# Gated products of two feed forwards in 512 columns instead of 256, on one Trainium2 core

## The chip, the cores and the metric

The kernel runs on one NeuronCore of one Trainium2 chip. The metric is the device time of one execution in microseconds (us). Five engines work side by side: PE (matmuls; PEld is its weight load), DVE and ACT (elementwise work, both can read the matmul banks), POOL (elementwise work on SBUF alone) and SP, which here issues every DMA.

## The reference

A two-layer transformer block on `x` of 128 sequences x 32 tokens x 256 features, with a context of 128 x 257 x 256. Each of the six steps adds to `x`, after a layer norm:

```python
x = x + L0_xattn(ln(x), ctx)      # 16 heads, 257 context tokens, biases, RMS norm of q and k
x = x + L0_attn(ln(x))            # differential attention with rotary positions
x = x + L0_ffn(ln(x))             # C: silu(x @ w1.T) * (x @ w2.T) @ w3.T, 704 features, weights through NF4
x = x + L1_xattn(ln(x), mask, ctx)  # 32 heads, self part and context part
x = x + L1_attn(ln(x))            # 16 heads of 16, causal
x = x + L1_ffn(ln(x))             # F: 8 experts, all applied, weighted by a router
# L1_ffn: gate = x @ Wg[e]; up = x @ Wu[e]; h = silu(gate) * up; out = sum_e w[e] * (h @ Wd[e]), 256 features
```

silu(a) is computed as a * (1 + tanh(a/2)) / 2, the halving being folded into later factors.

## The kernel before

The tokens are cut into 32 groups of 128 (4 sequences). Each step of the reference is a Python generator over groups: `A_prep`, `rowpass` (maxima of the scores, written to `mx`), `pvpass` and `pv` (exponentials `P`, their remainders `Pl`, products with `V`, copies `Uc`), `attn_fin`, `B_gen`, `C_gen`, then `D_prep`, `D_self`, the same `rowpass`/`pvpass`/`attn_fin` for layer 1, `E_gen`, `E_att` (the last attention, in tiles of 32x32 of the matmul array), `F_gen` and `F_down`. `C_gen` and `F_gen` take two groups at a time, so 256 tokens, 16 times each.

Numbers are kept to more than half precision by pairs: a value and its remainder, each in 16 bits. So a feed forward's hidden tile `hid` is written in float32, its upper halves are read as bfloat16, and POOL subtracts them from `hid` to give the remainder (`hidl` in C, `fhl` in F).

**What sets the order.** A planner (`pipeline`, `Stream.step`, `Est`) advances the generators one step (one `yield`) at a time, always the one with the smallest key. `Est.note` places each instruction into the first hole of its engine's estimated timeline after its operands are ready, with estimated costs from `Est.cost`. At the end every engine's instructions are sorted by estimated start, and that order is pinned for PE, ACT, DVE, POOL and the DMAs. The planner also counts matmul columns in stretches of `TICK` (3413 ns): where a stretch lacks columns (under `WARM` = 3060, pro rata), the streams in `HEAVY` (`ctx`, `F`, `Fd`) are pulled ahead, else held back.

**Banks.** PE writes eight banks of 128 x 512 float32. `tk()` gives a step the bank that is estimated to be free first; a step may take several.

**The gated products.** In F (`F_gen`) each expert has two feature tiles of 128. For each, 12 matmuls of 256 columns fill one bank: gates in columns 0 to 255, ups in 256 to 511. Then

```python
nc.scalar.activation(t, ps[:, :256], AF.Tanh, scale=0.5 * IWS)
nc.vector.scalar_tensor_tensor(t, t, 1.0, ps[:, :256], ALU.add, ALU.mult)
nc.vector.tensor_tensor(hid[:, ft], t, ps[:, 256:512], ALU.mult)
nc.gpsimd.tensor_tensor(hl[:, ft], hid[:, ft], hid.bitcast(BF)[:, ft, 1::2], ALU.subtract)
```

with `t` the tile `glu_t` of 128 x 256 float32 (two buffers). Each tile is one step of the stream. `F_down` multiplies `hid` and `hl` by the expert's third matrix (two times 6 matmuls of 256 columns) and adds into `xt`; it runs as a stream of its own, at most two experts behind. C is alike with 6 feature tiles (five of 128 and one of 64), 8 matmuls per tile, and its down product in the same generator.

All instructions are recorded by one helper, so every line of the profile names L290, and groups are told apart by the names of their tiles.

Of the kernel before, what the change touches and what calls it, by code (L numbers as in the profile page):

```python
# [12 lines left out]
F32 = mybir.dt.float32  # L13
F16 = mybir.dt.float16
BF = mybir.dt.bfloat16
AF = mybir.ActivationFunctionType
ALU = mybir.AluOpType
# [17 lines left out]
IWS = 1.0 / WS  # L35
# [55 lines left out]
FT = [128] * 5 + [64]  # L91
# [274 lines left out]
class Body:  # L366
# [140 lines left out]
    def ln_T(self, xts, pool, tag=None):  # L507
        nc = self.nc
        n = len(xts)
        mv = self.sm.tile([128, 2, 2], F32, name="bmv")  # L510
        for t in range(n):
            st = self.sm.tile([128, 6], F32, name="bst")
            nc.vector.bn_stats(st, xts[t])
            nc.vector.bn_aggr(mv[:, t, :], st)
        rs = self.sm.tile([128, 2], F32, name="brs")
        self.rsqrt(rs[:, :n], mv[:, :n, 1], 1e-5)
        hs = []
        nm = self.sm.tile([128, 2], F32, name="bnm")
        for t in range(n):
            nc.gpsimd.tensor_scalar(nm[:, t:t + 1], mv[:, t, 0:1], rs[:, t:t + 1], -1.0, ALU.mult, ALU.mult)  # L520
            h = pool.tile([128, 256], F32, name=f"lnh{t}", tag=tag, bufs=tag and n)
            nc.scalar.activation(h, xts[t], AF.Identity, bias=nm[:, t:t + 1], scale=rs[:, t:t + 1])
            hs.append(h)
        yield "end"
        ps = self.tk()
        for t, h in enumerate(hs):
            for k in range(2):
                nc.tensor.transpose(ps[:, (k * n + t) * 128:(k * n + t) * 128 + 128], h[:, k * 128:k * 128 + 128], self.ident)
        hT = pool.tile([128, 2, 2, 128 * n], F16, name="hT")
        self.split_ps(ps[:, :256 * n], hT[:, 0].rearrange("p k t -> p (k t)"), hT[:, 1].rearrange("p k t -> p (k t)"))  # L530
        return hT
# [624 lines left out]
    def setup_C(self):  # L1156
        nc, T = self.nc, self.T
        yield from self.need(("set", "A"))
        w1T = [self.w0.tile([128, 2, 704], BF, name=f"ffn{i}") for i in range(2)]
        self.w12T = w1T  # L1160
        self.w3T = self.w0.tile([128, 6, 256], BF, name="ffn3")
        w3d = self.dr.tile([88 * 2048], BF, name="w3d")
# [2 lines left out]
        for wi in range(3):  # L1165
# [3 lines left out]
            a = self.nf.tile([88, 32], F32, name="nfa")  # L1169
# [3 lines left out]
            ps = self.tk()  # L1173
# [25 lines left out]
            sc = self.nf.tile([88, 2048], BF, name="nfs")  # L1199
# [4 lines left out]
            for n in range(4):  # L1204
                ps = self.tk()
# [7 lines left out]
            if wi < 2:  # L1213
                for k in range(2):
                    ps = self.tk().bitcast(BF)
                    for r in range(8):
                        nc.tensor.transpose(ps[:, r * 88:r * 88 + 88], wq[:, r * 256 + k * 128:r * 256 + k * 128 + 128], self.identb[:88, :88])
                    nc.vector.tensor_copy(w1T[wi][:, k, :].rearrange("p (s r) -> p r s", r=8), ps[:, :704].rearrange("p (r s) -> p r s", r=8))
                    yield "end"
            else:  # L1220
                nc.sync.dma_start(w3d.rearrange("(p n) -> p n", p=88), wq)
                w3 = self.nf.tile([128, 2, 704], BF, name="nfw3", tag="nfs")
                nc.sync.dma_start(w3, w3d.rearrange("(k p f) -> p k f", k=2, p=128))
                for ft in range(6):
                    ps = self.tk().bitcast(BF)
                    for k in range(2):
                        nc.tensor.transpose(ps[:FT[ft], k * 128:k * 128 + 128], w3[:, k, ft * 128:ft * 128 + FT[ft]], self.identb)
                    nc.vector.tensor_copy(self.w3T[:FT[ft], ft, :], ps[:FT[ft], :256])
                    yield "end"

    def C_gen(self, g):
        nc = self.nc
        yield from self.need(("B", 2 * g), ("B", 2 * g + 1), ("set", "C"))
        xts = [self.xt[2 * g], self.xt[2 * g + 1]]
        hT = yield from self.ln_T(xts, self.cw, "glu_t")
        yield "end"
        hid = self.cw.tile([128, 6, 256], F32, name="hid")
        hl = self.cw.tile([128, 6, 256], F16, name="hidl")
        for ft in range(6):
            n = FT[ft]  # L1240
            ps = self.tk()
            for u in range(2):
                seq = [(k, a) for k in (0, 1) for a in (0, 1)]
                for i, (k, a) in enumerate(seq):
                    nc.tensor.matmul(ps[:n, u * 256:u * 256 + 256], self.w12T[u][:, k, ft * 128:ft * 128 + n], hT[:, a, k, :], start=(i == 0), stop=(i == 3))
            t = self.cw.tile([128, 256], F32, name="glu_t", bufs=2)
            nc.scalar.activation(t[:n], ps[:n, :256], AF.Tanh, scale=0.5)
            nc.vector.scalar_tensor_tensor(t[:n], t[:n], 1.0, ps[:n, :256], ALU.add, ALU.mult)
            nc.vector.tensor_tensor(hid[:n, ft], t[:n], ps[:n, 256:512], ALU.mult)
            nc.gpsimd.tensor_tensor(hl[:n, ft], hid[:n, ft], hid[:n].bitcast(BF)[:, ft, 1::2], ALU.subtract)  # L1250
            yield "pe" if ft < 5 else [hl]
        hv = hid.bitcast(BF)
        for tt in range(2):
            ps = self.tk()
            for ft in range(6):
                n = FT[ft]
                nc.tensor.matmul(ps[:, :256], hv[:n, ft, 1 + tt * 256:tt * 256 + 256:2], self.w3T[:n, ft, :], start=(ft == 0), stop=False)
                nc.tensor.matmul(ps[:, :256], hl[:n, ft, tt * 128:tt * 128 + 128], self.w3T[:n, ft, :], start=False, stop=(ft == 5))
            nc.vector.scalar_tensor_tensor(xts[tt], ps[:, :256], 0.5, xts[tt], ALU.mult, ALU.add)
            yield "pe"  # L1260
# [302 lines left out]
    def F_gen(self, g):  # L1563
        nc = self.nc
        yield from self.need(("E", 2 * g), ("E", 2 * g + 1), ("set", "F"))
        xts = [self.xt[self.NH + 2 * g], self.xt[self.NH + 2 * g + 1]]
        hT = yield from self.ln_T(xts, self.fw, "glu_t")
        w = self.router(hT)
        yield [hT]
        for e in range(8):  # L1570
            yield from self.need(*[("Fd", g * 8 + e - 2)] * (g * 8 + e > 1))
            hid = self.fw.tile([128, 2, 256], F32, name="fhid", bufs=2)
            hl = self.fw.tile([128, 2, 256], F16, name="fhl", bufs=2)
            for ft in range(2):
                ps = self.tk()
                for u, nm in enumerate((f"wg{e}", f"wu{e}")):
                    self.mm_feat(ps[:, u * 256:u * 256 + 256], self.W[nm], ft * 128, 128, lambda k: hT[:, 0, k, :], lambda k: hT[:, 1, k, :])
                t = self.fw.tile([128, 256], F32, name="glu_t", bufs=2)
                nc.scalar.activation(t, ps[:, :256], AF.Tanh, scale=0.5 * IWS)
                nc.vector.scalar_tensor_tensor(t, t, 1.0, ps[:, :256], ALU.add, ALU.mult)  # L1580
                nc.vector.tensor_tensor(hid[:, ft], t, ps[:, 256:512], ALU.mult)
                nc.gpsimd.tensor_tensor(hl[:, ft], hid[:, ft], hid.bitcast(BF)[:, ft, 1::2], ALU.subtract)
                yield "pe"
            self.fh[g * 8 + e] = (hid, hl, w)
            self.mark("Fu", g * 8 + e)

# [190 lines left out]
```

## Time and profile before

| | |
|---|---|
| median of 3 runs | 3372.8 us (3371.24 to 3373.25) |
| the profiled execution | 3372.91 us, its span 3371.1 us |
| mean granted PE clock | 0.937 of full speed |
| busy: PE, DVE, ACT, POOL | 3022.6, 2451.2, 2246.3, 2104.3 us |
| tanh of 256 columns (ACT, `glu_t`) | 352, 134.7 us |
| scalar_tensor_tensor (DVE, `glu_t`) | 352, 145.1 us |
| product (DVE, `fhid` and `hid`) | 256 and 96 |
| subtraction (POOL, `fhl` and `hidl`) | 256 and 96 |

In a line of the profile, "out<-in shape xcount" is followed by the busy time of the group in us, the mean ns of one, and after the second bar the idle time of the engine just before these instructions with what ended most of it. In windows, each engine has its busy us and its instructions in brackets; after the engines come the granted clock of PE, the share of DMA and GB/s.

### The profile page before, as it was taken

The numbers are of one execution on the slowest core, as the hardware profiler recorded it, in microseconds if no ns is written. First come the engines' busy times: TensorE is split into PE (matmuls) and PEld (weight loads), VectorE is DVE, ScalarE is ACT, GpSimd is POOL, SyncE is SP. The second block draws the span as 40 slices with busy tenths as digits, with TensorE's granted clock in tenths as the row PEclk, the third lists the DMA queues.
The fourth block names the chain that finished last, engine by engine and source line by source line (L and its number), as shares of the span: only waits on it lengthen the run. The fifth ranks groups of instructions, "written<-read, shape, count | busy, mean of one in ns | idle before, by whom it ended". The sixth has DMA issues, their size and how long they took to land. (4 is left out here: it accounts for less than half of the span.)

```text
span 3371.1 us, 106946 instructions
## 1 busy us (share of the span) xinstructions
PE 3022.6 (90%) x41537; PEld 2271.9 (67%) x41537; DVE 2451.2 (73%) x6084; ACT 2246.3 (67%) x6477; POOL 2104.3 (62%) x2537
## 2 busy tenths in 40 slices
PE   3888999999999999998777999889989889989899
PEld 1455776666766666665555777667777777777677
DVE  4787666766667666666767778777888788787866
ACT  2455888878887787786666656666676666656562
POOL 1354787777777777775454756556666656656463
PEclk9899999999999999999876999889999899988889
DMA  4565777777777777776565444544454445445420
GB/s 105 156 178 156 207 220 213 223 214 209 217 222 215 220 204 206 211 219 168 142 163 135 111 107 98 126 111 113 110 133 100 121 106 123 107 98 122 107 60 14
DMA packets 687849, 511.64 MB, mean 152 GB/s; under 512 B 224396, under 2 KB 675340, under 8 KB 687340
## 3 DMA queue, kind: packets, MB, share of 16 engines
q1 hardware_dynamic: 687340, 504.80, 55.1%
q8 instruction: 326, 5.34, 0.7%
q14 instruction: 183, 1.50, 0.2%
HBM read 319.86 MB, written 180.19 MB: 148 GB/s over the span
## 5 line engine op out<-in xcount | busy, mean ns | idle before, releaser
L290 POOL TENSOR_TENSOR Pl<-P 128x512 f16<-128x512 f32 x768 | 805.9, 1064 | 241.3 <-ACT P L290 232.4
L290 DVE TENSOR_REDUCE mx<-bank 128x2 f32<-128x512 f32 x768 | 479.8, 679 | 28.2 <-PE bank L290 25.2
L290 ACT ACTIVATE P<-bank 128x512 f32<-128x512 f32 x768 | 438.6, 599 | 89.1 <-PE bank L290 63.1
L290 ACT COPY Uc<-bank 32x68 f32<-32x68 f32 x1536 | 314.7, 205 | 108.0 <-PE bank L290 88.3
L290 DVE TENSOR_TENSOR vv<-bank,vv 128x256 f16<-128x256 f32 x512 | 215.2, 424 | 145.2 <-ACT vv L290 139.7
L290 POOL TENSOR_TENSOR fhl<-fhid 128x256 f16<-128x256 f32 x256 | 156.5, 612 | 250.2 <-DVE fhid L290 238.8
L290 ACT CAST vv<-bank 128x256 f16<-128x256 f32 x512 | 203.3, 402 | 156.9 <-DVE vv L290 84.9
L290 PE MATMUL bank<-V,P 128*128 128x68 f16 (+1 forms) x4096 | 295.5, 197 | 10.4 <-DVE mx L290 3.9
L290 PE MATMUL bank<-V,Pl 128*128 128x36 f16 (+1 forms) x3072 | 280.8, 191 | 11.3 <-POOL Pl L290 9.3
L290 PEld LDWEIGHTS <-Kst 97*128 97x128 f16 x4096 | 232.8, 100 | 78.1 <-issue 51.2
L290 PEld LDWEIGHTS <-P 128*128 128x128 bf16 x4096 | 258.1, 100 | 24.5 <-issue 7.9
L290 ACT ACTIVATE glu_t<-bank 128x256 f32<-128x256 f32 x352 | 134.7, 383 | 192.3 <-PE bank L290 170.1
L290 PEld LDWEIGHTS <-Pl 128*128 128x128 f16 x3072 | 235.0, 98 | 37.0 <-POOL Pl L290 21.8
L290 DVE SCALAR_TENSOR_TENSOR glu_t<-glu_t,bank 128x256 f32<-128x256 f32 x352 | 145.1, 412 | 116.4 <-ACT glu_t L290 115.2
L290 PEld LDWEIGHTS <-ch 128*128 128x128 f16 x2048 | 191.7, 99 | 56.1 <-issue 27.2
L290 PE MATMUL bank<-QstD,Kst 97*128 97x128 f16 x2048 | 200.4, 228 | 27.8 <-DVE rbt L290 5.5
L290 PEld LDWEIGHTS <-hT 128*128 128x128 f16 x1536 | 138.5, 102 | 107.7 <-issue 30.5
L290 POOL TENSOR_TENSOR kk<-kb,kk 128x512 f16<-128x512 f32 x128 | 146.0, 1160 | 94.0 <-ACT kk L290 92.7
L290 PE MATMUL bank<-khf,eh 32*128 32x256 f16 (+1 forms) x1536 | 162.7, 284 | 46.4 <-DVE mx L290 10.2
L290 POOL TENSOR_TENSOR cl<-ct,ch 128x1024 f16<-128x1024 f32 x64 | 136.6, 2135 | 44.8 <-ACT ch L290 42.7
L290 DVE SCALAR_TENSOR_TENSOR xt<-bank,w,xt 128x256 f32<-128x256 f32 x256 | 120.0, 472 | 21.5 <-PE bank L290 20.1
L290 PEld LDWEIGHTS <-eh 32*128 32x128 f16 (+1 forms) x1536 | 53.1, 93 | 121.9 <-issue 107.9
(483 smaller groups left out, 9098.2 us busy)
## 6 DMA issues: line engine op xcount, KB each, us to landing
Kst<-kd SPq DMA_DIRECT2D x384, 256.0 KB
kd<-kk SPq DMA_DIRECT2D x128, 512.0 KB
vd<-vv SPq DMA_DIRECT2D x256, 136.0 KB
V<-vd SPq DMA_DIRECT2D x64, 544.0 KB
vd<-vv SPq DMA_DIRECT2D x256, 132.0 KB
V<-vd SPq DMA_DIRECT2D x64, 528.0 KB
ct<-in_ctxm SPq DMA_DIRECT2D x64, 512.0 KB
khf<-kd SPq DMA_DIRECT2D x128, 256.0 KB
```

The source lines that it names most:

```text
L290: r = f(*a, **k)
```

## The change

The gates of two feature tiles go into one bank and their ups into another; so tanh, the two steps on DVE and the subtraction on POOL handle 512 columns at once. F then has one step of 24 matmuls per expert instead of two of 12, C three of 16 instead of six of 8. C's sixth feature tile becomes a full one: the transposed weights get 768 columns, of which the last 64 are set to zero by two memsets; its down product reads 64 rows as before. The three instructions move into a helper `glu`. The tiles `glu_t` (and the layer norm's `lnh`, which shares their buffers) grow to 512 columns, and the scratch for dynamic DMAs is set to 8192 bytes.

```diff
-            h = pool.tile([128, 256], F32, name=f"lnh{t}", tag=tag, bufs=tag and n)
+            h = pool.tile([128, 512], F32, name=f"lnh{t}", tag=tag, bufs=tag and n)[:, :256]
...
-        w1T = [self.w0.tile([128, 2, 704], BF, name=f"ffn{i}") for i in range(2)]
+        w1T = [self.w0.tile([128, 2, 768], BF, name=f"ffn{i}") for i in range(2)]
+        for t in w1T:
+            nc.vector.memset(t[:, :, 704:], 0.0)
...
+    def glu(self, t, ps, out, sc):
+        nc = self.nc
+        nc.scalar.activation(t, ps[0], AF.Tanh, scale=sc)
+        nc.vector.scalar_tensor_tensor(t, t, 1.0, ps[0], ALU.add, ALU.mult)
+        nc.vector.tensor_tensor(out, t, ps[1], ALU.mult)
...
 # C_gen
-        for ft in range(6):
-            n = FT[ft]
-            ps = self.tk()
+        for f2 in range(3):
+            f = slice(2 * f2, 2 * f2 + 2)
+            ps = [self.tk() for _ in range(2)]
             for u in range(2):
...
+                for ft in range(2):
+                    seq = [(k, a) for k in (0, 1) for a in (0, 1)]
+                    for i, (k, a) in enumerate(seq):
+                        nc.tensor.matmul(ps[u][:, ft * 256:ft * 256 + 256], self.w12T[u][:, k, (2 * f2 + ft) * 128:(2 * f2 + ft) * 128 + 128], hT[:, a, k, :], start=(i == 0), stop=(i == 3))
+            t = self.cw.tile([128, 512], F32, name="glu_t", bufs=2)
+            self.glu(t, ps, hid[:, f].rearrange("p f t -> p (f t)"), 0.5)
+            nc.gpsimd.tensor_tensor(hl[:, f], hid[:, f], hid.bitcast(BF)[:, f, 1::2], ALU.subtract)
+            yield "pe" if f2 < 2 else [hl]
...
 # F_gen
-            for ft in range(2):
-                ps = self.tk()
-                for u, nm in enumerate((f"wg{e}", f"wu{e}")):
-                    self.mm_feat(ps[:, u * 256:u * 256 + 256], self.W[nm], ft * 128, 128, lambda k: hT[:, 0, k, :], lambda k: hT[:, 1, k, :])
...
+            ps = [self.tk() for _ in range(2)]
+            for u, nm in enumerate((f"wg{e}", f"wu{e}")):
+                for ft in range(2):
+                    self.mm_feat(ps[u][:, ft * 256:ft * 256 + 256], self.W[nm], ft * 128, 128, lambda k: hT[:, 0, k, :], lambda k: hT[:, 1, k, :])
+            t = self.fw.tile([128, 512], F32, name="glu_t", bufs=2)
+            self.glu(t, ps, hid.rearrange("p f t -> p (f t)"), 0.5 * IWS)
+            nc.gpsimd.tensor_tensor(hl, hid, hid.bitcast(BF)[:, :, 1::2], ALU.subtract)
+            yield "pe"
...
-    nc = bacc.Bacc("TRN2", target_bir_lowering=False, num_devices=1)
+    nc = bacc.Bacc("TRN2", target_bir_lowering=False, num_devices=1, dynamic_dma_scratch_size=8192)
```

More of the change, by code (lines that the diff above doesn't have):

```diff
@@ L1217, in setup_C @@
                         nc.tensor.transpose(ps[:, r * 88:r * 88 + 88], wq[:, r * 256 + k * 128:r * 256 + k * 128 + 128], self.identb[:88, :88])
-                    nc.vector.tensor_copy(w1T[wi][:, k, :].rearrange("p (s r) -> p r s", r=8), ps[:, :704].rearrange("p (r s) -> p r s", r=8))
+                    nc.vector.tensor_copy(w1T[wi][:, k, :704].rearrange("p (s r) -> p r s", r=8), ps[:, :704].rearrange("p (r s) -> p r s", r=8))
                     yield "end"
@@ L1238, in C_gen @@
         hl = self.cw.tile([128, 6, 256], F16, name="hidl")
-        for ft in range(6):
-            n = FT[ft]
-            ps = self.tk()
+        for f2 in range(3):
+            f = slice(2 * f2, 2 * f2 + 2)
+            ps = [self.tk() for _ in range(2)]
             for u in range(2):
[L1243 to L1251, printed above, removed]
+                for ft in range(2):
[6 more added lines that the diff above has]
+            yield "pe" if f2 < 2 else [hl]
         hv = hid.bitcast(BF)
@@ L1573, in F_gen @@
             hl = self.fw.tile([128, 2, 256], F16, name="fhl", bufs=2)
-            for ft in range(2):
-                ps = self.tk()
-                for u, nm in enumerate((f"wg{e}", f"wu{e}")):
-                    self.mm_feat(ps[:, u * 256:u * 256 + 256], self.W[nm], ft * 128, 128, lambda k: hT[:, 0, k, :], lambda k: hT[:, 1, k, :])
[L1578 to L1583, printed above, removed]
+            ps = [self.tk() for _ in range(2)]
[6 more added lines that the diff above has]
+            yield "pe"
             self.fh[g * 8 + e] = (hid, hl, w)
```

## The prediction

> **What bounds the kernel now.** I read the page's busy line first, then the windows by stage, then one-microsecond windows, then the groups that the change touches, then DVE's order of time. The page:
>
> ```profile
> PE 3022.6 (90%) x41537; PEld 2271.9 (67%) x41537; DVE 2451.2 (73%) x6084; ACT 2246.3 (67%) x6477; POOL 2104.3 (62%) x2537
> ```
>
> PE leads, but 90% is an average. The windows by stage (PE, PEld, DVE, ACT, POOL busy, then the granted clock) part it:
>
> ```profile
> 400.00:1500.00 1100.00, 1058.91 (x11821) 762.34 (x11820) 740.96 (x1890) 880.32 (x2483) 830.55 (x970) 0.99 0.73 215
> 1500.00:1800.00 300.00, 236.54 (x2984) 167.71 (x2984) 207.11 (x462) 194.00 (x568) 159.25 (x195) 0.82 0.62 162
> 1800.00:3330.00 1530.00, 1390.29 (x23749) 1118.05 (x23748) 1203.55 (x2988) 963.23 (x2878) 924.11 (x1162) 0.92 0.44 106
> 3330.00:3371.10 41.10, 34.42 (x312) 28.56 (x309) 26.43 (x86) 7.95 (x22) 10.20 (x18) 1.00 0.04 14
> ```
>
> From 400 to 1500 (attention of layer 0 with the first feed forward, C) PE sets the pace: 41 us idle, full clock. From 1800 to 3330 (layer 1, with the experts, F) PE loses 140 us idle, and 113 us more to a lower clock (its busy time times one less the clock, summed over one-microsecond windows). DVE is 79% busy there, and not evenly: in 674 of the 1530 one-microsecond windows it is at 0.97 or more, and 72 of the 140 and 55 of the 113 us fall in these. Four windows in a row show how:
>
> ```profile
> 2413.00:2414.00 1.00, 0.45 (x4) 0.17 (x4) 1.00 (x3) 0.95 (x5) 1.00 (x1) 1.00 0.31 66
> 2414.00:2415.00 1.00, 0.73 (x4) 0.23 (x4) 1.00 (x2) 1.00 (x4) 0.05 (x1) 1.00 0.31 68
> 2415.00:2416.00 1.00, 0.78 (x8) 0.69 (x8) 1.00 (x3) 0.60 (x2) 0.00 (x0) 0.92 0.27 63
> 2416.00:2417.00 1.00, 1.00 (x6) 0.70 (x5) 0.90 (x3) 0.00 (x0) 0.22 (x1) 0.50 0.82 187
> ```
>
> DVE is full, PE waits for its maxima (0.45, 0.73), and then PE's clock is halved. The lower clock comes in 40 stretches of 3.4 us or small multiples, 251 us in all: 74 pieces of 3.4 us, each costing 113/74 = 1.5 us. So one DVE queue costs twice.
>
> **The change part by part.** Per expert, two tanh, two scalar_tensor_tensor, two products and two POOL subtractions of 256 columns become one each of 512; C's 96 become 48 likewise. The durations, from the page's groups:
>
> ```profile
> L290 POOL TENSOR_TENSOR Pl<-P 128x512 f16<-128x512 f32 x768 | 805.9, 1064 | 241.3 <-ACT P L290 232.4
> ...
> L290 ACT ACTIVATE P<-bank 128x512 f32<-128x512 f32 x768 | 438.6, 599 | 89.1 <-PE bank L290 63.1
> ...
> L290 POOL TENSOR_TENSOR fhl<-fhid 128x256 f16<-128x256 f32 x256 | 156.5, 612 | 250.2 <-DVE fhid L290 238.8
> ...
> L290 ACT ACTIVATE glu_t<-bank 128x256 f32<-128x256 f32 x352 | 134.7, 383 | 192.3 <-PE bank L290 170.1
> ...
> L290 DVE SCALAR_TENSOR_TENSOR glu_t<-glu_t,bank 128x256 f32<-128x256 f32 x352 | 145.1, 412 | 116.4 <-ACT glu_t L290 115.2
> ```
>
> and DVE's groups by form:
>
> ```profile
> L290 DVE TENSOR_TENSOR fhid<-glu_t,bank 128x256 f32<-128x256 f32 x256 | 107.3, 419 | 11.9 <-DVE glu_t L290 0.5
> L290 DVE SCALAR_TENSOR_TENSOR kk<-bank,kk 128x512 f16<-128x512 f32 x128 | 86.4, 685 | 24.9 <-ACT kk L290 24.4
> ```
>
> *DVE.* By durations an expert falls from 2x(412+419) = 1662 to 685+680 = 1365 ns (680: products of 512 from a bank), 297 less. Where DVE is full, neighbours overlap, so the time from start to start counts (start, duration):
>
> ```profile
> 2511.37 0.41 DVE L290 SCALAR_TENSOR_TENSOR glu_t<-glu_t,bank 128x256 f32<-128x256 f32 x1
> 2511.81 0.42 DVE L290 TENSOR_TENSOR fhid<-glu_t,bank 128x256 f32<-128x256 f32 x1
> 2512.15 0.68 DVE L290 TENSOR_TENSOR qkT<-bank,qkT 128x512 f16<-128x512 f32 x1
> 2512.75 2.47 DVE L290 TENSOR_REDUCE mx<-bank 128x2 f32<-128x512 f32 x4
> ```
>
> A pair takes 2512.15 - 2511.37 = 0.78 us. At 512 the first needs 0.685 + 0.03 (the second depends on it, as here) and the second 0.60 (qkT's start to the next): 1.315. Two old pairs less one new is 0.245 us. If all overlapped by 0.06 (mx: 4 in 2.47, where one lasts 0.68) it would be 0.18; if nothing did, 0.30. I take 0.245, measured on these very instructions. 120 experts lie before 3330: 29 us. On the path goes the share of windows in which DVE is full, 674/1530 = 44%: **13 us** (10 to 16 by the bounds; all 36 if DVE paced the whole stage).
>
> *ACT.* 2x383 - 599 = 167 ns, 120 times: 20 us. ACT is at 0.95 or more, DVE not being full, in 262 of 1530 windows: **3.5 us**. Two tanh one after the other took 0.81 us, no less than 2x0.383, so I count nothing off. [...]
>
> *POOL.* 2x612 - 1064 = 160 ns, 120 times: 19 us. Full alone in 197 of 1530 windows: **2.5 us**.
>
> *The other stages.* C saves the same per pair of tiles on engines that PE outruns in need: DVE is full in 314 of its 1100 windows, but PE lost only 10 us in those. **1 us** (0 to 5). 1500 to 1800: PE's largest waits there are for mx (9.9 us), QstD's load (4.9) and weights (4.3), none of which the change touches: 0. The last 41 us are paced by PE (34.4 busy): tanh and the first product now run beside the ups' matmuls, after which product and subtraction take 0.68+1.06 against 0.38+0.41+0.42+0.61 for the last tile before: 0, within 0.5.
>
> *PE and the banks.* The matmuls are as many and as wide (C's sixth tile now has 128 rows for 64; rows do not show in the durations, 606 against 612 ns in POOL's subtraction). One tile took 12 matmuls, 1.3 us, in one bank; now 24, 2.6 us, in two banks at once. Bank time per expert, without queueing: 2x(1.3+0.38+0.41+0.42) = 5.0 us before; gates 1.3+0.60+0.68 and ups 1.3+0.68 after, 4.6. No new shortage. A new wait is possible where the first down matmul, which could start on the first tile's half, now needs both: PE waited 15.4 us for fhid in this stage. I keep that sum. Behind the longer tanh stand P's exponentials, behind the longer subtraction Pl's; neither new piece is longer than those, so nobody's worst wait grows.
>
> *Coarser filling.* The planner pulls F ahead when PE's current 3.4 us lack columns. It had 256 pieces of 3072 columns for that, now 128 of 6144, of which one may fill a stretch twice and leave the next thin. Below by nothing (a piece spread over two stretches serves both); above, 20 more slow pieces, 30 us. I take 3 pieces, **4.5 us** against the change, near the lower end, since matmuls are placed one by one into holes. [...]
>
> *Less thin time.* If a lighter DVE queue spares 2 of 74 slow pieces (DVE's load falls by 29/1204 = 2.4%): **3 us**.
>
> *Memsets and scratch.* Two small memsets in the start-up: under 0.5 us on DVE. [...]
>
> Sum: 13+3.5+2.5+1+3-4.5 = 18.5 us. The profiled execution took 3372.9 us (span 3371.1), the median is 3372.8, so nothing is to be converted: **3354 us**.
>
> **The rivals.** *Slower by clumps.* Every engine's order is written out from the planner's estimates, so all of it is dealt anew, and F's doubled pieces leave more thin stretches. For: the clock falls on thin windows, not on gaps; F and its down products are the only filler in this stage. Against: estimates are placed matmul by matmul. Against 23 us of gain at 1.5 us each, 15 more slow pieces (on 74) cancel the change, and from 20 it is slower. At 30: 3373-23+45 = 3395 us. *Nothing.* In DVE's full windows PE is still 89% busy (72 of 674 idle); the freed time goes to waits for P and Uc on ACT (15.2 and 11.4 us of PE's waits), and the new order scatters it: 3371 us. *More.* Full DVE windows set off the slow clock; if 20 of 74 slow pieces go, 30 us on top of 18: 3325 us. *Not as said:* if the ups' first matmul waited for the second bank to be drained, PE would show waits ahead of wu; the 4.6 against 5.0 us speaks against it.
>
> **How the numbers follow.** Forecast (3335 to 3366) 0.45, more 0.12, nothing 0.14, clumps 0.29. The measurement can tell about 0.2%, 6.7 us, from no change: faster 0.57, same 0.14, slower 0.29. The range runs from 3322 (DVE's 36 us, ACT, POOL and 3 slow pieces) to 3394 (some 30 slow pieces more); a tenth is left out on each side. The faster cases alone: 3325 to 3366.
>
> **What would show it.** Right: tanh near 600, both DVE forms near 680, POOL near 1060 ns, 176 each; DVE's sum in F's stage down by 30 to 36 us at equal PE busy; fewer full DVE windows; PE waits for mx below 15.7 us. Wrong: a clock under 0.92 from 1800 to the tail with more half-clock stretches; PE waits for fhid well over 15.4 us; or a longer 400 to 1800, where I expect no change.

## The result, and the profile after

After the change the kernel takes 3401.5 us (median of 6 runs, 3390.8 to 3409.4) against 3372.0: a ratio of 1.0087, 95% interval 1.0067 to 1.0107, so 29 us slower. The profiled execution took 3390.8 us, its span is 3389.0 us. The page's busy line:

```profile
PE 3032.6 (89%) x41537; PEld 2284.1 (67%) x41537; DVE 2397.2 (71%) x5734; ACT 2227.7 (66%) x6301; POOL 2081.5 (61%) x2361
```

The relief is there: DVE has 54 us less, ACT 19, POOL 23, with 350, 176 and 176 fewer instructions. The groups have the forecast durations (597, 680 and 1040 ns, 176, 176 and 128 of them):

```profile
L290 POOL TENSOR_TENSOR fhl<-fhid 128x512 f16<-128x512 f32 x128 | 133.1, 1040 | 215.0 <-DVE fhid L290 208.0
...
L290 ACT ACTIVATE glu_t<-bank 128x512 f32<-128x512 f32 x176 | 104.9, 597 | 103.8 <-PE bank L290 89.4
L290 DVE SCALAR_TENSOR_TENSOR glu_t<-glu_t,bank 128x512 f32<-128x512 f32 x176 | 119.7, 680 | 74.5 <-ACT glu_t L290 73.6
```

The windows by stage (columns as before) show where the time went nevertheless:

```profile
400.00:1500.00 1100.00, 1066.19 (x12058) 772.69 (x12055) 743.45 (x1842) 890.93 (x2480) 842.72 (x951) 1.00 0.75 218
1500.00:1800.00 300.00, 237.33 (x3063) 168.97 (x3060) 198.18 (x441) 194.56 (x577) 158.21 (x189) 0.80 0.62 158
1800.00:3330.00 1530.00, 1379.01 (x23113) 1107.28 (x23114) 1147.90 (x2706) 931.11 (x2697) 886.52 (x1017) 0.90 0.44 104
3330.00:3389.00 59.00, 47.24 (x620) 38.76 (x617) 32.45 (x86) 9.81 (x20) 13.12 (x15) 0.88 0.06 15
```

Until 1500 us the kernel is a little ahead (237 more matmuls than before in the stretch from 400 us, clock 1.00 for 0.99), and at 1800 us it leads by 328. In layer 1 it falls back: in the same 1530 us, 636 fewer matmuls, with a clock of 0.90 for 0.92. Summed over one-microsecond windows from 1800 to 41 us before the end, PE sat idle 157 us (before 140) and ran 308 us at half clock (before 251), although DVE is at 75% where it was at 79%. The cost of the lower clock, summed as in the prediction, is 133 us there for 113. Together that is 37 us lost in layer 1; with the lead at 1800 us, the profiled execution ends 18 us later than the one before (it is the fastest of the six).

What happens is seen in the one-microsecond windows around 2757 us, after the change (PE, PEld, DVE, ACT, POOL, clock, then the share of DMA and GB/s):

```profile
2756.00:2757.00 1.00, 0.76 (x5) 0.20 (x5) 0.93 (x5) 0.33 (x2) 0.63 (x1) 1.00 0.00 0
2757.00:2758.00 1.00, 0.00 (x0) 0.00 (x0) 0.83 (x6) 0.00 (x0) 0.00 (x0) 1.00 0.00 0
2758.00:2759.00 1.00, 0.04 (x1) 0.04 (x2) 0.87 (x3) 0.00 (x0) 0.00 (x0) 1.00 0.19 68
2759.00:2760.00 1.00, 0.58 (x4) 0.14 (x3) 0.99 (x2) 0.00 (x0) 0.22 (x1) 1.00 0.18 64
2760.00:2761.00 1.00, 0.77 (x6) 0.60 (x5) 1.00 (x3) 0.00 (x0) 0.81 (x1) 0.75 0.00 0
2761.00:2762.00 1.00, 1.00 (x7) 0.70 (x5) 1.00 (x3) 0.00 (x0) 0.00 (x0) 0.50 0.61 206
```

and in PE's order of time (start, duration; in brackets the idle time ahead and what ended it):

```profile
2754.18 0.38 PE L290 MATMUL bank<-hT,wu0l 128*128 128x256 f16 x2
...
2756.03 0.73 PE L290 MATMUL bank<-khf,eh 32*128 32x256 f16 x4
2758.96 0.37 PE L290 MATMUL bank<-khf,eh 32*128 32x256 f16 x2 [2.19 <-DVE glu_t L290]
2759.75 0.37 PE L290 MATMUL bank<-khf,eh 32*128 32x256 f16 x2 [0.42 <-DVE fhid L290]
2760.35 0.91 PE L290 MATMUL bank<-hT,wg1h 128*128 128x256 f16 x4 [0.23 <-DVE mx L290]
```

The last ups of expert 0 (`wu0l`) ran at 2754; then `rowpass` (khf) waits for the bank that held that expert's gates until DVE, busy with the router's small steps, has read it at 2758. No matmul of F stands in the order until `wg1h` at 2760, so nothing fills the gap; the granted clock goes from 1.00 to 0.50 at 2760.5 us, and the next 24 matmuls begin under it (the row of two `wg1l` at 2761.05 reads 0.63 us, that of two `wu0l` at 2754.18 0.38).

One place proves little, so I counted this over layer 1. From PE's order of time, cut into 448 stretches of 3.41 us from 1800 us, 150 had no gate or up matmul before; after, 241. And this absence goes with the clock: of 38 falls of the clock in layer 1 before, 20 had no matmul of F (gates, ups or down) in the 4 us ahead, while only 10% of all full-clock microseconds have that; after, 28 of 44, and 16% of all.

PE's waits in layer 1 (total us, times, longest), two of them before:

```profile
PE bank L290 <- DVE fhid L290: 15.4, 15, 2.6
PE bank L290 <- DMA QstD<-ed: 1.9, 2, 1.4
```

and after:

```profile
PE bank L290 <- DMA QstD<-ed: 24.1, 6, 6.6
PE bank L290 <- POOL Pl L290: 16.6, 35, 1.0
PE bank L290 <- DVE mx L290: 15.9, 51, 1.3
PE bank L290 <- DVE glu_t L290: 13.9, 8, 3.4
...
PE bank L290 <- DVE fhid L290: 4.2, 11, 0.9
```

The wait for fhid fell from 15.4 to 4.2 us, but one for glu_t's bank (13.9 us, none before) took its place: together 18.1. Part of this is a change of name: before, a bank held gates and ups and was freed by the product into `fhid`; now the gates' bank is freed by the step before it. The 24.1 us for QstD's load look like a cause, but the kernel of before is the exception with its 1.9: two new orders of it without any edit (`before_n1` and `before_n2` below) have 11.1 and 17.7, and C alone, the fastest kernel here, 16.4.

### The profile page after: what moved, and what is told of

Read it like the earlier page. It is cut to its first block, busy times and chain, and to the rows that moved or that the text cites. A ratio compares the mean times of both kernels' runs of the same rounds, so it can differ in the third digit from the quotient of the medians.

```text
span 3389.0 us, 106178 instructions
## 1 busy us (share of the span) xinstructions
PE 3032.6 (89%) x41537; PEld 2284.1 (67%) x41537; DVE 2397.2 (71%) x5734; ACT 2227.7 (66%) x6301; POOL 2081.5 (61%) x2361
## 4 chain that ended last, share of the span: by engine, by line
PE 54%; DVE 17%; DMA 10%; ACT 8%; issue 5%; POOL 4%; SPq 1%; DVEq 0%; ACTq 0%; POOLq 0%
PE bank L290 54%; DVE mx L290 4%; POOL Pl L290 1%; SPq L290 1%; DVE vv L290 1%; ACT P L290 1%; DMA ed<-el 1%; DVE nfmk L290 1%; ACT Uc L290 1%; DMA QstA<-mT 1%; ACT vv L290 1%; DMA QstD<-ed 1%; DVE rbt L290 1%; DVE dS L290 1%; POOL Tm L290 1%
## 5 line engine op out<-in xcount | busy, mean ns | idle before, releaser
L290 PE MATMUL bank<-V,P 128*128 128x68 f16 (+1 forms) x4096 | 305.0, 197 | 11.9 <-DVE mx L290 3.0
L290 PE MATMUL bank<-V,Pl 128*128 128x36 f16 (+1 forms) x3072 | 289.0, 193 | 22.1 <-POOL Pl L290 20.9
L290 POOL TENSOR_TENSOR fhl<-fhid 128x512 f16<-128x512 f32 x128 | 133.1, 1040 | 215.0 <-DVE fhid L290 208.0
L290 PEld LDWEIGHTS <-ch 128*128 128x128 f16 x2048 | 191.4, 98 | 50.8 <-issue 22.3
L290 ACT ACTIVATE glu_t<-bank 128x512 f32<-128x512 f32 x176 | 104.9, 597 | 103.8 <-PE bank L290 89.4
L290 DVE SCALAR_TENSOR_TENSOR glu_t<-glu_t,bank 128x512 f32<-128x512 f32 x176 | 119.7, 680 | 74.5 <-ACT glu_t L290 73.6
L290 DVE TENSOR_TENSOR hT<-bank,hT 128x256 f16<-128x256 f32 (+1 forms) x160 | 75.3, 472 | 89.9 <-ACT hT L290 88.9
```

Of the source, the lines that this page charges most:

```text
L290: r = f(*a, **k)
```

## The experiments

Three theories. *Step*: F's step of 24 matmuls is too coarse to fill PE's thin stretches. *Width*: the 512-column chain or its two banks cost. *Deal*: any edit deals the pinned order anew, and this is one bad deal. In all that follows "half clock" is the time at half clock in layer 1 (from 1800 us to 41 us before the end, before: 251 us), and "bare" the number of the 448 stretches without a gate or up matmul (before: 150), both from the run's profile.

### Parts of the change, and step against width

`c_only` has the whole change in C and F as before; `f_only` the reverse.

> The first feed forward (C) as after the change, the experts (F) as before. C runs where PE is 96% busy, so if the loss of 29 us comes from F's coarser steps, this stays within 8 us of before (3372) and layer 1 from 1800 us on has the same 0.92 clock. If any new dealing of the order costs time, layer 1 differs too, by anything up to 30 us, although nothing in it was edited.

Measured: 3347.2 us, ratio 0.9920 (0.9893 to 0.9947); half clock 233, bare 138. That is 25 us less than before, more than the 8 us that were expected if only F mattered.

> F as after the change, C as before. If the loss comes from F (coarser steps, later banks), about 3400 us with PE's clock near 0.90 in layer 1. If it comes from C, about 3372 us or, by the terms of the forecast, 3355 us.

Measured: 3416.4 us, ratio 1.0136 (1.0104 to 1.0167); half clock 333, bare 257. So the loss is F's, and C for its part gained, in this order.

`f_two_steps`, against `f_only`:

```diff
+            t = self.fw.tile([128, 512], F32, name="glu_t", bufs=2)
             for u, nm in enumerate((f"wg{e}", f"wu{e}")):
+                ps[u] = self.tk()
                 ...
+                if u == 0:
+                    nc.scalar.activation(t, ps[0], AF.Tanh, scale=0.5 * IWS)
+                    nc.vector.scalar_tensor_tensor(t, t, 1.0, ps[0], ALU.add, ALU.mult)
+                    yield "pe"
+            nc.vector.tensor_tensor(hid.rearrange("p f t -> p (f t)"), t, ps[1], ALU.mult)
```

> F in 512 columns, but in two steps of the planner as before: the 12 gate matmuls with tanh and the first DVE step, then the 12 ups with the product and the subtraction. C as before. If the coarse step of 24 matmuls is the cost, this gets the forecast's gain: 3345 to 3365 us. If the 512-wide chain itself or the two banks cost, about 3400 us, as with one step.

Measured: 3378.5 us, ratio 1.0018 (1.0002 to 1.0034); half clock 247, bare 158. The step back to 12 matmuls takes 38 us off, but the forecast's gain isn't there: neither expectation holds in full.

`f_one_step_256`, against before, is one yield moved out of a loop:

```diff
             for ft in range(2):
                 ...
-                yield "pe"
+            yield "pe"
```

> All instructions of before, F's two tiles of an expert in one step of the planner (24 matmuls) instead of two. If the coarse step is the cost, 3395 us or more, since nothing is saved on DVE. If the width or the banks are, about 3372 us.

Measured: 3430.5 us, ratio 1.0164 (1.0121 to 1.0208); half clock 332, bare 242. Its windows by stage show the same picture as after the change, with not one instruction altered:

```profile
1800.00:3330.00 1530.00, 1366.80 (x22846) 1094.66 (x22846) 1156.87 (x2882) 948.34 (x2831) 905.16 (x1130) 0.89 0.44 106
```

The step alone costs 59 us here; *width* can't explain that.

### Is a new order worth this much by itself?

`before_n1` and `before_n2` alter one estimate of the planner by 2 ns:

```diff
-    LAT = {"pe": 196.0, "act": 150.0, "dve": 135.0, "pool": 75.0, "dma": 910.0}
+    LAT = {"pe": 196.0, "act": 150.0, "dve": 135.0, "pool": 77.0, "dma": 910.0}   # n1; n2: "act": 152.0
```

> The program of before; only the planner's estimate of POOL's latency is 77 instead of 75 ns, so that the order is dealt anew without a reason. If orders scatter at random by as much as the parts measured so far differ (24 to 59 us), this can land anywhere from 3345 to 3400 us; if the step's size is the cause, it stays within 10 us of 3372.

> A second new dealing without a reason: the estimate of ACT's latency is 152 instead of 150 ns. The same bounds: within 10 us of 3372 if orders scatter little, 3345 to 3400 us if they scatter much.

Measured: 3377.6 us (0.9994 to 1.0034) and 3370.1 us (0.9971 to 1.0001); half clock 241 and 230, bare 156 and 152. Little scatter, for this kernel.

`f_four_steps_256` gives each tile a `yield "pe"` after its gates too (the bank is held until its second half is placed):

> The instructions of before; each of F's tiles in two steps (6 gate matmuls, then 6 ups with the elementwise work), so four steps of 1536 columns per expert. If coarser steps lose because the planner has fewer and larger pieces to fill PE's thin stretches with, finer ones gain: 3350 to 3368 us, and less half-clock time than 251 us in layer 1. If two steps were only a lucky order, no direction: 3372 give or take the scatter.

Measured: 3373.2 us, ratio 1.0003 (0.9987 to 1.0020); half clock 228, bare 87. Far fewer bare stretches and no gain. So *step* holds between 24 and 12 matmuls, not below; I had expected it to go on.

### The change with the step put back, under three orders

`c_f_two_steps` is the whole change with F as in `f_two_steps`.

> The whole change, but with F in two steps of 12 matmuls (the kernel after the change with the one yield put back). By the parts (C alone 24 us less than before, F in two steps 7 more) 3355 us; if C's gain was a lucky order of layer 1, 3378.

Measured: 3368.8 us, ratio 0.9985 (0.9966 to 1.0004); half clock 245, bare 158. Between the two.

C alone, twice more under a new order:

> C alone in 512 columns, dealt anew by a POOL latency of 77 ns in the planner. If C's 24 us are its own, 3340 to 3358 us; if they were a lucky order, 3365 to 3380.

> C alone in 512 columns, dealt anew by an ACT latency of 152 ns. As the run before: 3340 to 3358 us if C's gain is its own, 3365 to 3380 if it was a lucky order.

Measured: 3351.2 us, ratio 0.9938 (0.9919 to 0.9957), and 3387.3 us, ratio 1.0049 (1.0030 to 1.0067). Neither expectation holds for both: with C's edit the same two-nanosecond accidents span 40 us. So the step had to be tried under each order too:

> The kernel after the change, dealt anew by a POOL latency of 77 ns in the planner. If the step of 24 matmuls costs by itself, 3385 to 3430 us, above its partner with two steps; if the loss was an accident of the order, as likely below as above 3372.

> The whole change with two steps of 12 matmuls per expert, the same dealing. If the step's size is the cause, 3350 to 3380 us and at least 15 us below its partner; if not, no order between the two.

> The kernel after the change, dealt anew by an ACT latency of 152 ns. As for the other dealing: 3385 to 3430 us if the step costs by itself.

> The whole change with two steps per expert, dealt by the ACT latency of 152 ns. 3350 to 3385 us and at least 15 us below its partner if the step's size is the cause.

Measured, each as its ratio to before, beside the pairs from above:

| pair: 12 against 24 matmuls in a step | 12 | 24 | difference | half clock, us | bare |
|---|---|---|---|---|---|
| before, `f_one_step_256` | 1 | 1.0164 | 1.64% | 251, 332 | 150, 242 |
| `f_two_steps`, `f_only` | 1.0018 | 1.0136 | 1.18% | 247, 333 | 158, 257 |
| `c_f_two_steps`, after | 0.9985 | 1.0087 | 1.02% | 245, 308 | 158, 241 |
| the same, n1 (3353.8 and 3410.3 us) | 0.9936 | 1.0110 | 1.74% | 198, 329 | 156, 243 |
| the same, n2 (3406.0 and 3424.2 us) | 1.0102 | 1.0150 | 0.48% | 300, 307 | 170, 246 |

The intervals of the last two pairs: 0.9912 to 0.9960 and 1.0090 to 1.0130; 1.0074 to 1.0129 and 1.0132 to 1.0169. All five pairs have the same sign; the mean is 1.2%, 41 us. The n2 kernel with 12 matmuls was outside its expected 3350 to 3385, the gap of its pair (18 us) just within what was expected. So *step* is settled as an average, and *deal* is true as well: over three orders the unedited kernel spreads over 9 us, the one after the change over 21, C alone over 43 and the two-step kernel over 56. A single pair, that of n2 above all, doesn't stand clear of that.

The way from the step to the time can be seen in the profiles. In the traces of before and after, the 66 falls of PE's clock from 100 us on lie on a grid of 3.413 us, within 0.01 us. I weighted each matmul's columns by its rows over 128, a choice of mine, and added them up by the stretches of this grid, from 400 us to 41 us before the end. Before, 58 stretches that began at full clock ended with a fall: half of them have under 2005 columns, and 52 under 2750. Of the 687 that kept the clock, 682 have 2750 or more. After, 50 of 58 and 674 of 677. Over all 20 profiles, 88% of the falls lie below 2750 and 99% of the others at or above. So call a stretch under 2750 "thin", and count these in layer 1; beside them stands how much more the lower clock costs there with 24 matmuls (summed as in the prediction, one profile each), and the difference of the pair by the ratios:

| pair | thin with 12, with 24 | more lost to the clock, us | difference, us |
|---|---|---|---|
| before, `f_one_step_256` | 65, 90 | 27 | 55 |
| `f_two_steps`, `f_only` | 66, 88 | 40 | 40 |
| `c_f_two_steps`, after | 61, 78 | 28 | 34 |
| the same, n1 | 48, 99 | 57 | 59 |
| the same, n2 | 77, 84 | 9 | 16 |

So most of what the step costs is lost to the clock. `f_four_steps_256` has 52 thin stretches, not far below the 65 of before: fewer bare stretches are not yet fewer thin ones.

### Does the step cost through the planner's rule?

`before_noheavy` and `one_step_256_noheavy` set `HEAVY = ("ctx",)`.

> The program of before with F and its down products taken out of the planner's rule that pulls them ahead when a stretch of PE lacks columns (the rule is kept for ctx). It is the base for the next run. If the rule is worth what its wording says, 3390 to 3430 us with more half-clock time than 251 us in layer 1; if not, about 3372.

> F's two tiles in one step (24 matmuls, 256 columns), and the same rule taken away. If the coarse step loses through the rule (pieces too large to fill thin stretches with), it is within 10 us of the run before it. If it loses by itself, since 24 matmuls placed at once push other streams' matmuls back, it is 40 to 70 us slower than the run before it, as with the rule (59).

Measured: 3392.4 us, ratio 1.0064 (1.0045 to 1.0083), half clock 327, bare 194; and 3407.4 us, ratio 1.0106 (1.0083 to 1.0129), half clock 373, bare 240. Without the rule the coarse step costs 15 us, not 59; the 10 us of the first reading are just missed. The number of bare stretches is telling: with the rule, the fine step has 150 and the coarse one 242; without, 194 and 240 (thin ones 65 and 90; 89 and 93). By these counts the rule spreads F's work over PE's time if the pieces are small, and hardly if they are of 24. One pair under one order: that most of the cost runs through the rule is likely, given the scatter, rather than shown.

### Is DVE on the path at all?

`f_no_product`, against before (the product with the ups is left out on 248 of 256 columns; scalar_tensor_tensor now writes `hid` itself, so `glu_t` is free sooner too):

```diff
-                nc.vector.scalar_tensor_tensor(t, t, 1.0, ps[:, :256], ALU.add, ALU.mult)
-                nc.vector.tensor_tensor(hid[:, ft], t, ps[:, 256:512], ALU.mult)
+                nc.vector.scalar_tensor_tensor(hid[:, ft], t, 1.0, ps[:, :256], ALU.add, ALU.mult)
+                nc.vector.tensor_tensor(hid[:, ft, :8], hid[:, ft, :8], ps[:, 256:264], ALU.mult)
```

> The program of before, steps and banks and widths as they were, but F's product with the ups is done on 8 of its 256 columns only (the rest of the product is left out). DVE saves about 0.42 - 0.17 = 0.25 us 240 times before the tail, 60 us. If DVE's load goes onto the path by the share of full windows, 44%, as forecast: 26 us, 3346 us. If DVE is busy but not what PE waits for, 3362 to 3378 us. If DVE paces layer 1, 3312.

> The same with the order dealt anew by a POOL latency of 77 ns (its partner without the edit took 3378 us). Forecast's share: 3352 us; DVE not waited for: 3368 to 3384; DVE paces: 3318.

Measured: 3355.8 us, ratio 0.9947 (0.9925 to 0.9969), and 3403.3 us, ratio 1.0077 (1.0045 to 1.0109). Layer 1 in the two:

```profile
1800.00:3330.00 1530.00, 1390.35 (x23918) 1122.93 (x23916) 1150.24 (x3050) 967.65 (x2891) 931.81 (x1172) 0.92 0.44 106
```

```profile
1800.00:3330.00 1530.00, 1369.18 (x23033) 1097.83 (x23034) 1116.86 (x2928) 956.38 (x2861) 916.25 (x1149) 0.91 0.45 107
```

DVE has 53 and 87 us less than the 1203.55 before in this stretch (in the second fewer experts were done, too), and the kernels are 18 us faster than before and, by the ratios (1.0077 and 1.0014), 21 us slower than the partner `before_n1`. That excludes DVE as the pace of layer 1 (both would be near 3315). The two have 62 and 73 thin stretches. Between the forecast's 44% and nothing it decides nothing, except that the accident of the order outweighs 60 us of DVE work.

## Why the prediction was wrong

The forecast was 3354 us (3322 to 3394); measured were 3401. The direction was wrong, and the rival that came true was *clumps* (0.29, priced at 3395 us).

**The step that failed: coarser filling.** It was put at 4.5 us (3 slow pieces, bounds 0 and 30 us); the five pairs put it at 16 to 59 us, 41 on average. That is some 36 of the 47 us between forecast and measurement. Half-clock time rose by 57 us (308 less 251), 17 pieces of 3.4 us for 3, at a cost of 20 us (133 less 113), and PE's idle time by 17 more. The reason for choosing the lower end, that the planner places matmuls one by one into holes, was the mistake. It places them into the first holes after the step is chosen, so that pieces chosen together stay together: 241 bare stretches for 150, and 78 thin ones for 65 (before) or 61 (`c_f_two_steps`). With four steps instead of two nothing was gained, so the cost is not a smooth one. A possible reason, not tested: a piece of 3072 columns is about what the planner wants in one stretch (3060), and one of 6144 is two. "Less thin time", 3 us for 2 slow pieces spared, had the wrong sign for the same reason; with the step kept, in `f_two_steps`, half-clock time fell by one piece (251 to 247 us).

**DVE's 13 us.** The durations were right to 1% (680 and 686 ns for 685 and 680), and so was the saving (`f_two_steps`: 1169 for 1204 us in layer 1, 34 less, where 30 to 36 were foretold). What failed is the factor of 44%, the share of one-microsecond windows in which DVE is full. In `f_two_steps`, with 34 us less work, there are more of these (728 for 674), and the time is 7 us up. An engine that is full for a microsecond needn't be what PE waits for in it; in those windows PE was 89% busy, as the prediction said under *nothing* and then didn't use. ACT's and POOL's 6 us were reckoned in the same way and share the fault. ACT's term had a wrong reading besides. The row of two tanh in 0.81 us lies in the tail (at 3335 us), where the second began 0.06 us after the first had ended. Where two stood back to back, at 369.9 and 461.4 us, they took 0.64 us together, an overlap of 0.10 and 0.11, and of 195 pairs of P's exponentials the typical one overlaps by as much. With 0.1 us of overlap counted off, the term is an estimated 1.4 us, not 3.5.

The pairs that differ in F's width, at 12 matmuls a step (and in which 12: gates and ups of a tile, or gates of two tiles and then their ups), gave by the ratios 6 (before, `f_two_steps`), 22, -1 and 18 us (C alone against `c_f_two_steps` under three orders) against 512 columns. That is within the scatter of the orders: a cost of the width is not shown, and no gain either. A piece of such a cost may be the gate bank, which is now freed only by the longer scalar_tensor_tensor (680 ns after for 412 before). PE's longest waits in layer 1 of `f_two_steps`:

```profile
PE bank L290 <- DVE mx L290: 25.2, 57, 3.1
PE bank L290 <- DVE glu_t L290: 18.7, 10, 3.9
```

The 18.7 us for glu_t and 4.0 for fhid make 22.7, 7 more than the 15.4 before; but `before_n2`, with not one instruction altered, has 22.3 for fhid alone. The forecast reckoned bank time without queueing (4.6 for 5.0 us) and said "no new shortage"; in the place shown above, at 2758 us, it is the queue on DVE ahead of the read that the bank waits for.

**C's 1 us.** C alone measured 25 us less than before, then 18 less, then 18 more. Where it gained, the stage from 400 to 1500 us got further:

```profile
400.00:1500.00 1100.00, 1067.90 (x12025) 771.99 (x12022) 742.09 (x1840) 889.87 (x2477) 841.22 (x949) 0.99 0.74 218
```

(12025 matmuls for 11821). But the other order that gained has 11912, the slow one 11822, and `f_one_step_256`, whose C is as before, 11914. How much of the gain is C's and how much the order's stays open; three orders don't settle it.

**Right** were the unchanged start (2692 matmuls by 400 us for 2679) and tail (304 in the last 41 us for 312), nearly the sum of the fhid wait (15.4 before, 18.1 with its successor), and the rows that tell of the outcome: the clock in layer 1 at 0.90, under 0.92, was named as the sign of the rival. Of lesser weight: in the windows at 2413 us, 0.91 us of PE's idle time ended with DVE's qkT and only two waits of 0.2 us with its maxima, and the lower end of the range, 3322, is 3326 by the terms named for it. Every DMA issue is SP's, before and after (2978 each).

On the clock itself: in the 3.413 us ahead of a fall in layer 1, PE was 0.56 busy on average before (39 falls by the clock's own records) and 0.59 after (46). The longest idle gap in that time was 1.05 us in the median before and 0.77 after, at most 3.14 and 2.92; 18 of the 39 and 30 of the 46 had none of 1 us. So in these two traces thin work came ahead of the falls, and often without a long gap, as *clumps* had it.

The fastest kernel measured is C alone (ratio 0.9920); the whole change with the yield put back reached 0.9936 under one order and 1.0102 under another.

## What to carry to other kernels

Where a planner interleaves streams, the size of a step is a parameter of its own: merge instructions if that saves fixed costs (here 680 + 686 ns of DVE per expert for 2 x (412 + 419)), but keep the yields where they were, and count how evenly the filler then lies on the busiest engine. The share of time in which a second engine is full was no measure here of what it costs the first (in `f_two_steps`, 34 us less of DVE's work and 7 us more time); ask what the first waits for. And before an effect of half a per cent is believed, deal the order anew two or three times for nothing: here that alone spread a kernel over 9 to 56 us in three orders.

## What the runs showed of the hardware

In layer 1 before, PE's granted clock fell 39 times, after 3.413 us in which PE was 0.56 busy on average, and it stood at 0.50 in 40 stretches of 3.4 to 13.7 us, 251 us in all. PE's busy share doesn't part the stretches of 3.413 us that ended in a fall from the others: from 400 us on before, falls came after up to 1.00 busy, and the clock was kept at as little as 0.47. Columns weighted by rows part most of them: 52 of the 58 with a fall have under 2750, and 5 of the 687 others. Without the weight, 23 of the 58 have under 2750 and a tenth over 4627. Why that is so, no run here shows. At 0.50 the 256-column matmul's row reads 421 ns (before, `wg5h` from 2416.2 us on), and at 1.00 272 (`wdn4h` from 2419.53 us on).
